# Routed experts beside a scan on one core: rows scattered unscaled, two rankings of the experts, and three late experts of the last block combined on chip

## The chip, the cores and the metric

The kernel runs on one core of a Trainium2 chip. A core has TensorE (PE in the profile; its weight loads are shown apart as PEld), VectorE (DVE), ScalarE (ACT), GpSimd (POOL) and SyncE (SP), each with its own instruction stream, and DMA queues. The metric is the device time of one execution in microseconds. Three runs of the kernel before took 468.14, 471.61 and 472.38 us, so the median is 471.61.

## The reference

The input is 16 sequences of 256 tokens with 128 features, 4,096 rows in all. Four sublayers follow one another, each on a layer norm without gains and added to its input:

```python
x = x + attention(_layernorm(x))          # layer 1
x = x + ffn(_layernorm(x))
x = x + selective_scan_block(_layernorm(x))  # layer 2
x = x + ffn(_layernorm(x))
```

The attention multiplies its softmaxed weights, summed over the keys, with v at the query's own place; these sums are 1, so what remains is a product with two matrices. The scan block keeps 16 states per feature over the sequence, with `delta` through a softplus, and ends with a matrix, a skip term `u * D` and a bias. The ffn is a mixture of eight experts of 128 x 512 and 512 x 128 with a relu between them. Each token goes to two:

```python
gate_logits = x @ gate_w
top_vals, top_idx = jax.lax.top_k(gate_logits, TOP_K)
top_w = jax.nn.softmax(top_vals.astype(jnp.float32), axis=1)
h = jax.nn.relu(jnp.einsum('td,edf->etf', x, w1))
expert_out = jnp.einsum('etf,efd->etd', h, w2)
```

and its output is the sum of its two experts' rows, weighted with `top_w`.

## The kernel before

The 4,096 rows are held on chip as eight blocks of 512 tokens (`xs_[b]`, four tiles of 128 tokens each). In what follows "layer 1" is attention, the first ffn and the scan (the *mixer*); "layer 2" is the second ffn. Layer 1 takes its blocks in the sets [0], [1], [2,3], [4,5], [6,7], layer 2 in [0,1], [2,3], [4,5], [6], [7].

For each set the ffn goes through four steps.

*Routing* (`choose`, `route`, L1156 and L1330): VectorE finds the two best experts of each token and their softmax shares `p`; small bf16 matmuls count tokens, so that each token gets a place in the list of its expert. Each expert has a *room* (`SLOTS`): n pieces of K rows. Then each token's row is normalized, multiplied with its share and written, once for each of its two experts, into a DRAM buffer `slots` at its place: ScalarE or VectorE makes `row` from x, and GpSimd scatters 128 rows with one indirect DMA (L880). Because the expert's relu commutes with a positive factor, the share may be applied to the input. Set [0] of layer 1 goes without DRAM: its rows are dealt to the experts by matmuls with marks (`spot`, `dealt`; tile `u` of `ramp` compared with places).

*Experts* (`experts`, L1389): for each expert the room is fetched (`xs<-slots`), transposed, multiplied with w1 (tiles `ps_b` and `ps_B` from `xsT`), put through the relu (`h`), multiplied with w2 (`ps_y`), transposed back (`yr`) and written to a DRAM buffer `ys`. Rows of the eight experts alternate in `slots` and `ys`, so that a room is read in pieces of 512 bytes.

*Collection* (`collect`, L1446): for each block GpSimd gathers each token's two rows (`yy<-ys,of`, L892, four gathers for each of the two), and VectorE or GpSimd adds them to x as a whole, 128x512.

*What follows*: the mixer in layer 1 (`arrive`), the transposed output to DRAM in layer 2 (`finish`).

In layer 2 the first set ranks the experts by load (`ranking`), so that the rooms can fall from the busiest expert to the least busy. The weights are loaded again from DRAM in that order, by registers that SP reads (`load_experts`, L934 to L940). In layer 1 all rooms of a set are equal.

The mixer (L1492) normalizes and transposes x to `u`, computes `delta`, runs the scans of the 16 states in four groups (exp and tanh on ScalarE, products and scans on VectorE, broadcasts of B and C by bf16 matmuls), and ends for each block with two matmuls into one sum: `wsd_s` (the output matrix times D) with u, 512 columns, and `wsh_s` with the scan's last 180 steps of both sequences, 360 columns.

The order of the instructions on each engine is fixed before the chip runs: all operations are jobs of a plan, with the duration that the plan believes, and a stored list of ranks (`ORDER`) and choices of engine decides which job goes next on which engine. On SP the order of the DMA issues is fixed in the same way; a DMA there that waits holds back those behind it. Where the plan leaves TensorE without work for 0.5 or more, it puts one matmul with a blank tile for every 0.26 of the gap (L1705): these *fillers* compute nothing.

After the last block the kernel tests whether a room was too small or the scan's cut was too short; then a general path computes all of it again, without routing.

Of the kernel before, what the change touches and what calls it, by code (L numbers as in the profile page):

```python
# [19 lines left out]
P = 128  # L20
# [12 lines left out]
    {  # L33
        "first": ((88, 2),) * 8,
        1: ((84, 2),) * 8,
        2: ((108, 3),) * 8,
    },
    {
        "first": ((126, 3), (112, 3), (108, 3), (98, 3), (96, 3), (88, 3), (126, 2), (117, 2)),
        1: ((98, 2), (91, 2), (88, 2), (80, 2), (84, 2), (75, 2), (70, 2), (128, 1)),  # L40
        2: ((126, 3), (117, 3), (110, 3), (104, 3), (108, 3), (96, 3), (90, 3), (126, 2)),
    },
)
RANKED = (2,)
UNIT = 2
JOIN = 2

COLD = 5.0
# [14 lines left out]
    "c-qZZ2V4_p|G(!F2uWCBZ^GVNMD}nMWhmmpRjsY4t)oufI_lQiswi$nt>RvFf>K)%!~%*UB1=HoJFEa1cmE`Jxw{}(`+wi}^LZ0U"  # L63
    "a?kVJZ+?H@-|v>G_^I*=>c6NNCEAl^pxer^W>rkfI9&R;>iv%8rd7`B9lu02joA1NUDGqgsne+5m*>sC|3s_)i)v%K>WE364%f`z"
    "G%9VWd>|BeK0IC08FfuyS$#TV!ssUsJvZ9pw@tBaV2TlOKM(^Ype&9CWvPXsXYyKG+Pu%zXlZI1Sm&A}IY4CALbDer*&iR4gwV&l"
    "%_}jzc_s5zX!X3PvIWf#4x)X!&c}M*s#~aW*_FM4<>R>>-Ss7LRsE&oXUE3!i@n2)%YK;$2Ux%Q=KJd&AzO97EXmqll<=(G$|n86"
    "dYcDRExkEyN=&Uj^@^>Aca=O|2u`0WZ*KkZPp*nx>bjin<VsZC<o=9uRhFUFl+z=MPhNm~zw4pXzFM^_s$-IHUykn8ElEaxc^26-"
    "@4I$-U9_@v4^`W~w0Z1KeP?YmwJLUVr{|Jk*2t*vvi=>escnr%S2%5T@YvyUd1cK_&1T~j6D^|8^}R6ZVc4@5r`2UVu#9lkK^d>j"
    "<5raWMYj1fEzYZOy26KDMUnzv7Ki#3$Js3MGeWdkH_RQX!$+g^SGwX*L0g)m*&ht^hr`B{m+-Z+MtiQ=%kQlyO?ID9`_|x>g>x4a"
    "7{0aWT9KvwE7Mny<Gx<_BC^rwXq|G-%~+*L?XOC-N_X*TlWs>d*t>6dr4MgmZ>V5Cdl#UwvuaJIa7A;6SkO9NyAy2)R#I*_c4irG"  # L70
    "f$}i1aA)c7s#VilXwygk=1!Yh4K5@zA4WBp!hdS2*QXZDe|&PBD<YV-*P?Y!iDl#0qE3S>ix*QK?M<<E=x(XAp(VMh1?XG@R;LUe"
    "^+r5mvX*|O{~BSeh+)#r_1}t5_Zhr&a6Vyi`WybF4oh}yO!N4+5htCOsU-6w+usb|b1Ki@BBPCK;{T?1ty+gYBRIVexWd-=;yaSJ"
    "&s)c$pQk1Mu(kK>{gXydj2^f9i*!A>vkJ$Aory7?vCXs9d*QbqY<=vPD_5viZHRw+xyi_Maei$clW%G}<<Bhkhz`r&MH-;Cg^e&a"
    "U3gYoEtvixd0S^(bWqX_ezZ?DQW4gCxKZW)U-sXiwFV<^9XWugj&I$OH!^<jINSI_Rp(0X8CAy1J2}<+XY8MsQOzx+FI`ck!)UF1"
    "r{3=xWR>+`>d7lshLx35&odZn7Zx}mrDnxJanplDErz>)?7F~R3+C+aA5-pJSJA{omZhmanOZhgkCAfdi0_(u)pB)q^G@34(G14f"
    "eS4#Xe51_BB9U#NK~YP9t>|iZM^tyo*>WS%F&D1MxJN(sPW#RtZCBBJZJ^)!epUT0n_AeiD}P#^{fyO-2NJ+a(?751T|Dt?cbC&s"
    "Vc(n$QTC>HM#at;b;t51I;SD3MmT%!f%h}4>PBvxuFe>3;@b3@A8^VmYfe%~m6J|SeG|jhc2S6Tkp)nnb$DNx$-9k@&62&})9eDh"
    "ScjD#Mm+6S`}*KmrOj)ty&MV-D)rOH_rKCv)^PRbMmOGYj!yTV8??Q`+N`UlY#O%f5B};74O>|C*7x@ozso+too$4EyDPAtJ-2Le"
    "uTEEI%<mI*o7jdlVWH_fj=;E{yK8^RlKf4p9e+HX@qI@>qK&dre+c0=@TMCTa6xyst-wJ;H>2N&$y}<c%!q`U@CUzomIp^G>DPJt"
    "S!x=E$jI-zmAMAtYp?dBF3J<a_^i}!9^FgHm{tEc#Gh9&w{A|0ef5VbPi>8y1=e34J|A%@QR|nJJQv~V+30jzx^DxA@33*RbCs>%"  # L80
    "ef3A`HOopwyjkjeHH}(F$Ieng4b!X;HExa5f1%a}jGt%hF>5F+ZFknJV%x@_61{ioY8P?EddV{*+HUb(fS#Qbt)^2r^(WJ`)UPYu"
    ")JFWl;98WeIb=8Tk2<=R1-&Pa79=`8w;g#um40nvvTte-sCm{D_|vkM$>|}6bRG!cYgMZ0^S*OreBm=TH+%Z~Jcp5~?Y_@P(9st@"
    "2CsX<E{?mh@~%t6aDJ(4L*w;>xy$qNjg9mfd=Ae^*L+-(bAJ8d=)3ycVdKZQ%egm9ODFqhX5N_LFyCI_K3f0nvJ^FDW!RAzPKVo+"
    "&IIVELnF5YsV!Rmvh`YcsoiL^-lwHm!S_vG?p9glT3%@%v(D~K^6D*%ik-FG(>9-*)PGiwXO`l5rF63Hy$X+bo)u_IOW1QRTiI}<"
    "<_VqfqH_^joC>Np-yO~piB@y!^DI<vt(p<a79|+4%EN6Q+BDz2GK+27_hV+{U*BnPFSKTUHNV=Vhjk($xUov;CwT7HHq%es;o@7v"
    "s~x8lM&||AjNuQ<wZ6Bmwd>bY8~1<UXj(W%Ur`$cXWJOv-;lnhYT8?FUx$uYp|x^`un9G&o1Iu;t!dRW&g^Bb=_0hyX(rG0_x5<J"
    "W}lxb*X~)HAE-1pB;BQ^LG!O|{!7wateXuPjy1g47G;AAOE#v|-`IO4l;JX=Le)SmG4aUQQQ6kXA%1z9t<NK0dmq^jAGBJpuKxgd"
    "eXkawFZ5$JMr2mlKB{8c=h)_Zy$KD=PPGs%xvk#g-~MD_9aH;}d%czM@ozmdc5X7%n7k(1V&fu#xkh5jB_tPq;C45@tIXzkaGgr;"
    "`U-V}elJ1K5|2t9!%F4Ie79N)zMgFdqAF5lr;az799pBdl=r?p=s{9t<;`CXoASO{t7VrlBRG@0J_1I0K8Wt`_lI$swmu6BI^+PG"
    "R<t`R#ilQeDPFoWaTfD_W-45&V`fle={DiT+;e$tuyA_JGv2os@98-1FqqaFKEJbL>3+MFs}kA@zjoxM2@bBZ-Zv|~*-qnO412%B"  # L90
    "Hrl?39I;U2Nl)*kc{(>WG8$)ax|gm~8_)17zHBvazRBVuOO~Pjb<fxgT5}Y$rBU13yY<|T>gT@6y{t2fvzNc1KieD~H?c3yIG5%1"
    "EZC;L<sGZu9pMPV16%ccCfxd9<XECrYvkB!<h1ocr=`%<`N@intL=VX)*h7_ooi=p!&4c>U}btmTfv<omWIQ-a$8N>Cfiq*;mz*K"
    "X~Rn9R^2?n+niWz_x`eL{ozpO&1-+YWLh^$VDQqHpSVriI0n@^F|pk#E1}=9&or)NWV*op*e;vXrU5-JJxh-3Fk{-vL_ZWd-(`H2"
    "k@>2&TjXi*rq>P$e>>}7fV!t%UxR&U@8s&d;UV$g>F5|2Zpc2S=4zO^Jm5y+3zK*Htk~qyL5(?+wC+!_Zq6Cy`MkJ=^V`TyeWuXt"
    "&YapiOGBTs*#<0g<ztSzO#Mb4*Oi?TS!SZ4o^E#ZOhD4zQ=R+|Ixbw%HSS}*_Wf~Z>nrHuK4p{B+fH~UE>nKqtaR_P_PR4V=)GIP"
    "!Ikr-C#gjoJ>T&4m`N)*+szxBUi?zstQE)^-*auA<Lrx}7Gn-|ZG9f9D$<H~iw)(J4uc)c&AfL9uaDPpx~_b%G&X4U1Ad5jy|0kt"
    "-q%m7eTec@?E3E4PPX$n(aU-rFg1Mb6W;3N3jQ<IiG33%{1O-0xc2P#Mc2LUH4C!)1d=i2$+S8jbn2MmrUfI44!n=6D`;&|bw8)y"
    "MfYYF)pRR$)vNK;YU^v8rn%{zpSh*DMQ>#O<%u3}gHdkWyZcHxnY}jZ*J4i7EpLtfqkWEhOIbWuuiJ~hV{K6Q^&if?00DY0hVOmz"
    "w(r2s*FMAf{wuvbzY9&%5hrHsZXcB!Frs-!vd?v~)$Q@#yhiOE3(d+F)HQFI-@S##Q8iU@>%DG>IK7Hv8*S0w$rzhkaXC6o)ji8s"
    "`!Bs^j7RVnPN~uUeqGnob@xW?s`toU?B})Hci%{(+x}N#%V$Pprx$y2*!ij>)2t(qr7We8OpgM4w#&%LI@|8^R%NLE{xFwj+K}6m"  # L100
    "b#UGJVz!Frr07J=%-<$(E^!5ZPiC$>cICE-+9D&MvC_q=&c?IIp#PomyfstNq`8xn_PPi{-i^Qb^B4icKWSfnWuEpshKGMXO-KBa"
    "=BoRm!22z7$df~xYih~RD4J0_uHf#=@y4}b4=0M=y}F&4Z()!27mYJDP#W|4r2qBc5k6+ZsmEp;lr-B_g}@On;%JxdtZy7=+QdGx"
    "yla*QO+TGe7qCPrt6tNs!1LsF+YX1c?FNBPU%_hnsIm6g1-Z(n%9a$4aLcXI(=D#wS?k^4&KOZ*`&&}y{2h1Nf(s*Ou)a7J-V;=5"
    "`P4q4-{LJlR5<M0=6>%|UzTqL+sN`e7sJ_KZg8@&@au7ONDB*z{gWFQUT1pQv}Vx+x9Hik#V7Rl+Z)hgxUIJA$4R$lKR?^2v3_#!"
    ">)PnR%R2jnzwLTu3Uu|kbtp<>T=OyQvM-&@w&$T@l}_3ZQ*NSLbH51^?E9;{t@f*o)tW*1N!vbj^|Lw3#=Yep4jt^mESpJxfC&!u"
    "_j<e<oHm85F<l%mC!pg^x#5;03HD#!nfc|W!Yv&~&3er&Hy#Y)c(sHwV#d^Ud=anS!QbqV|0JrT#@hFbW6e=28?RYgY;T}n^*esh"
    "+f#V-iGLybGSv_*tJ;;?#RTx?(>iSLS`GI|w-ybT=8a5-_S(Yg$bBX;2j0eVis|qA3g-E?KhJwV&Eu78T5)&z_y-)N`nxw$=*&I4"
    "nhaG+6Gw5t#PeFdh8BM?nN!+Kv}|TAVpYGdJksWFbWPdEPrax`*`nI_smPJjoW9V~)4$rh{Hwd?rzM>5KH{xeU~?{qv)X@bwaNGe"
# [553 lines left out]
def tile_layers(  # L662
# [43 lines left out]
    def room(k, blocks):  # L706

        first = blocks == routed[k - 1][0]
        return SLOTS[k - 1]["first" if first else len(blocks)]
# [1066 lines left out]
```

## Time and profile before

| | |
|---|---|
| median of three runs | 471.61 us |
| the profiled execution | 467.84 us, its span 466.1 us |
| TensorE busy | 447.0 us (96%), of which fillers 31.2 |
| VectorE busy | 345.6 us (74%) |
| ScalarE busy | 268.3 us (58%) |
| GpSimd busy | 311.8 us (67%); 128 gathers 125.5, 120 scatters 120.6 |
| DMA | 55.37 MB in 74,917 packets |
| granted TensorE clock | 0.994 |

The profile is one execution. Nearly all operations are recorded by one helper, so that they share the line L772, and are told apart by their tiles: `ps_y<-h,w_s` is a matmul that writes a `ps_y` bank from `h` and a weight. An f32 matmul stands as two records. A record of a matmul covers its whole pass through the array, and the passes overlap: how much one takes of TensorE's time is read from the distance of their starts, or from the chain, which counts each moment once. The chain of the last-ending work is followed back from the end, at each step to what released it.

### The profile page before, as it was taken

The page shows a single profiled execution, that of the slowest core. Times are in us where ns is not written, and L with a number is a line of the kernel's source. Part 1 is how long each engine was busy: PE and PEld are TensorE (multiplying, and loading weights), DVE is VectorE, ACT ScalarE, POOL GpSimd, SP SyncE. Part 2 cuts the span into 40 slices and gives each one's busy share as a digit, 9 for nine tenths or more (in the row PEclk, how much of TensorE's full clock was granted, in tenths as well). Part 3 has the DMA queues.
Part 4 walks back from the last instruction along what each step waited for, and adds up shares of the span by engine and source line. Part 5 has one row for each costly group of instructions (what it writes and reads, how often), then busy time and mean ns, then how long its engine had stood idle before and what let it go on. Part 6 is the DMA issues. An engine that isn't in the chain of part 4 may idle for free.

```text
span 466.1 us, 8797 instructions
## 1 busy us (share of the span) xinstructions
PE 447.0 (96%) x2670; PEld 355.8 (76%) x2670; DVE 345.6 (74%) x1229; ACT 268.3 (58%) x621; POOL 311.8 (67%) x482
## 2 busy tenths in 40 slices
PE   8999999999999999989997999989999999999994
PEld 6889998866766667665665777677678877999993
DVE  4799999778697878999999998996786931223420
ACT  2124443577576854995889496797735534343310
POOL 8188787777673761276866776836785477778662
PEclk9999999999999999999999899999999999999999
DMA  5974234632352423236644322144225333543251
GB/s 155 340 244 135 71 122 134 166 107 66 108 155 67 114 78 96 65 106 195 188 121 142 93 73 76 53 120 132 69 58 146 114 113 90 135 125 91 78 164 45
DMA packets 74917, 55.37 MB, mean 119 GB/s; under 512 B 8184, under 2 KB 66800, under 8 KB 74864
## 3 DMA queue, kind: packets, MB, share of 16 engines
q1 hardware_dynamic: 66640, 38.35, 28.5%
q0 software_dynamic: 7936, 16.27, 12.1%
q8 instruction: 23, 0.38, 0.4%
q14 instruction: 30, 0.25, 0.2%
q10 hardware_dynamic: 288, 0.13, 0.1%
HBM read 28.95 MB, written 25.77 MB: 117 GB/s over the span
## 4 chain that ended last, share of the span: by engine, by line
PE 72%; DVE 16%; ACT 4%; issue 3%; POOL 2%; DMA 1%; POOLq 0%; DVEq 0%; ACTq 0%
PE ps_b L772 25%; PE ps_y L772 24%; PE ps_B L772 21%; DVE x L772 3%; DVE ps_B L772 2%; DVE stats L772 2%; PE ps_y L1705 2%; POOL yy L892 2%; DVE w L772 1%; DMA yy<-ys,of 1%; DVE th L772 1%; ACT th L772 1%; DVE rt L772 1%; ACT decay L772 1%; DVE u L772 1%
## 5 line engine op out<-in xcount | busy, mean ns | idle before, releaser
L892 POOL DMA_INDIRECT yy<-ys,of x128 | 125.5, 980 | 64.4 <-issue 37.2
L880 POOL DMA_INDIRECT slots<-row,to x120 | 120.6, 1005 | 49.5 <-issue 19.4
L772 PE MATMUL ps_y<-h,w_s 128*128 128x324 f32 (+13 forms) x552 | 145.2, 382 | 0.0
L772 PE MATMUL ps_B<-xsT,w_s 128*128 128x324 f32 (+9 forms) x352 | 112.8, 442 | 0.8 <-DVE w L772 0.4
L772 PEld LDWEIGHTS ps_y<-h,w_s 128*128 128x128 f32 x552 | 90.4, 190 | 20.3 <-issue 1.3
L772 PEld LDWEIGHTS ps_B<-xsT,w_s 128*128 128x128 f32 x352 | 61.7, 191 | 23.8 <-issue 3.2
L772 ACT ACTIVATE h<-ps_B 128x648 f32<-128x648 f32 (+9 forms) x62 | 43.8, 707 | 33.5 <-PE ps_B L772 33.1
L772 PE MATMUL ps_b<-xsT,w_s 128*128 128x176 f32 (+9 forms) x288 | 54.8, 316 | 1.2 <-ACT yr L772 1.2
L772 PEld LDWEIGHTS ps_b<-xsT,w_s 128*128 128x128 f32 x288 | 44.1, 190 | 2.7 <-ACT yr L772 1.5
L772 ACT COPY yT<-ps_y 128x324 f32<-128x324 f32 (+14 forms) x52 | 18.8, 362 | 36.0 <-PE ps_y L772 35.2
L772 ACT ACTIVATE th<-later,lneps,ha_s 128x112 f32<-128x112 f32 (+13 forms) x85 | 39.1, 507 | 0.2 <-DVE th L772 0.2
L772 ACT ACTIVATE h<-ps_b 128x352 f32<-128x352 f32 (+9 forms) x47 | 22.3, 474 | 26.0 <-PE ps_b L772 24.1
L772 PE MATMUL ps_b<-ident,yT 128*108 128x128 f32 (+11 forms) x177 | 34.4, 274 | 0.7 <-ACT yr L772 0.7
L772 ACT COPY xsT<-ps_b 128x324 f32<-128x324 f32 (+15 forms) x52 | 19.1, 372 | 26.6 <-PE ps_b L772 25.3
L772 ACT ACTIVATE decay<-delta,nea 128x108 f32<-128x108 f32 (+13 forms) x85 | 31.7, 412 | 2.7 <-DVE delta L772 2.6
L1705 PE MATMUL ps_y<-blank,ones_d 128*128 128x128 f32 x232 | 31.2, 293 | 1.3 <-DVE blank L772 1.3
L772 DVE TENSOR_TENSOR_SCAN w<-decay,ps_B 128x360 f32<-128x360 f32 (+7 forms) x40 | 31.0, 802 | 1.3 <-ACT decay L772 0.5
L1705 PEld LDWEIGHTS ps_y<-blank,ones_d 128*128 128x128 f32 x232 | 30.0, 208 | 1.6 <-DVE blank L772 1.3
L772 ACT COPY yr<-ps_b 108x384 f32<-108x384 f32 (+13 forms) x50 | 21.3, 425 | 16.8 <-PE ps_b L772 16.8
L772 ACT ACTIVATE row<-x,mp,rp 128x128 f32<-128x128 f32 x63 | 28.1, 488 | 3.6 <-DVE rp L772 2.0
L772 PE MATMUL ps_b<-ident,xs 108*128 108x108 f32 (+13 forms) x186 | 29.7, 256 | 0.1
L772 DVE TENSOR_SCALAR h<-ps_B 128x648 f32<-128x648 f32 (+6 forms) x26 | 21.3, 819 | 11.1 <-PE ps_B L772 10.8
(207 smaller groups left out, 792.2 us busy)
## 6 DMA issues: line engine op xcount, KB each, us to landing
w_s<-in_w SPq DMA_DIRECT2D x32, 256.0 KB
xs<-slots SPq DMA_DIRECT2D x27, 162.0 KB
ys<-yr SPq DMA_DIRECT2D x27, 162.0 KB
slots<-blank SPq DMA_DIRECT2D x2, 1280.0 KB
xT<-in_xT SPq DMA_DIRECT2D x8, 256.0 KB
yy<-ys,of POOLq DMA_INDIRECT x128
out_T<-xnT SPq DMA_DIRECT2D x8, 256.0 KB
slots<-row,to POOLq DMA_INDIRECT x120
```

What stands on the lines that cost most here:

```text
L772: return lambda: f(*[real(x) for x in a], **{n: real(x) for n, x in k.items()})
L880: inst = nc.gpsimd.indirect_dma_start(out=real(out), out_offset=bass.IndirectOffsetOnAxis(ap=real(rows), axis=0), in_=real(in_), in_offset ...
L892: nc.gpsimd.indirect_dma_start(out=real(out), out_offset=None, in_=real(in_), in_offset=bass.IndirectOffsetOnAxis(ap=real(rows), axis=0),)
L1705: nc.tensor.matmul(out=spare, lhsT=ones_d.real(), rhs=blank.real(), start=True, stop=True,)
```

## The change

- The rooms of the experts are set one set at a time. The experts are ranked in set [2,3] of layer 1 as well as in the first set of layer 2; the sets that follow use that ranking. The rooms of one set stand one behind the other in `slots` and `ys`, each in one piece.
- The ranking's tables hold a start and an end for each room, on all partitions. A token past its room's end is sent to spare rows behind the rooms.
- The first matrix of each expert is multiplied with I - 1/128 after loading (`centre`), eight matmuls of 512 columns, and the centred w1 and w2 are stored to DRAM (`w1c`, `w2c`); both reloads come from there. SP reads all eight registers in one step.
- Rows are scattered as x itself. The share times the reciprocal deviation (`share`) is applied at the collection: the first expert's rows, and all of layer 2, tile by tile with `scalar_tensor_tensor`; in layer 1 the second expert's rows are multiplied with it by ScalarE (or VectorE), tile by tile, and then added in one piece.
- For the last block of layer 2 three experts (`LATE`) are neither written nor gathered. Four mark matrices with the shares are built, transposed, and multiply the experts' rows on TensorE into the transposed output (`marks`, `finish`).
- The mixer scales u by 2D and adds the scan to its last 180 steps, and one matmul of 512 columns follows.
- Block 0's reciprocal deviations come from a power on GpSimd; marks of the first set may be made on ScalarE by two activations.
- The believed durations of transfers and the stored order are others.

```diff
+RANKED = ((1, 2), (2, 0))
+LATE = 3
@@ def load_experts(q)
+                pw = bank("B", P, FF)
+                matmul(pw, centre, into[0])
+                copy(into[0], pw)
+                move(w1c[r], into[0], 4 * P * FF, took=0.5, turn="centred")
+                move(w2c[r], into[1].rearrange("p c d -> p (c d)"), 4 * P * FF, took=0.5, turn="centred")
...
+            for f, t, of in ((first, into[0], [w1c]), (second, into[1], [w2c])):
+                plan.job([("SP", 0.55, f)], [t], of, late=-4.0 * P * FF, turn="weights", after=[seen])
@@ def choose(blocks, k)
-        V.tensor_tensor(rp, p, r.unsqueeze(1).to_broadcast([P, 2, n]), ALU.mult)
-        V.tensor_tensor(mp, p, m.unsqueeze(1).to_broadcast([P, 2, n]), ALU.mult)
+        share = new(f"share{n}", [P, 2, n], bufs=3)
+        V.tensor_tensor(share, p, r.unsqueeze(1).to_broadcast([P, 2, n]), ALU.mult)
@@ class Group
         def part(self, t, r):
-            n, c = self.room[r]
-            return t[0 : NE * n * c].rearrange("(p c e) w -> e p c w", e=NE, c=c)[r]
+            _, c = self.room[r]
+            return t[self.starts[r] : self.ends[r]].rearrange("(p c) w -> p c w", c=c)
@@ def marks(q, f)
+        for t in range(NTT):
...
+            for i, v in enumerate((hot[t], other)):
+                V.tensor_scalar(v, tail, f[:, i, t : t + 1], q.share[:, i, t : t + 1], ALU.is_equal, ALU.mult)
+            V.tensor_tensor(hot[t], hot[t], other, ALU.add)
...
+                for t in range(NTT):
+                    transpose(pt[:, ts(t, P)], hot[t][:, at : at + 1 + C * (K - 1) : C], hold=[m] if t == 0 else ())
+                copy(m, pt)
@@ def route(q, blocks)
+        if not q.dense:
+            past = small("rest", n, NE)
+            V.tensor_tensor(past, at[:, 0:n], spread(lies[:, 1], n), ALU.is_ge)
+            V.scalar_tensor_tensor(at[:, 0:n], past, BIG, at[:, 0:n], ALU.mult, ALU.add)
...
-                    either(
-                        ("ACT", "activation", (r[:, t, :], xs_[b][:, t, :], AF.Identity),
-                         dict(bias=m, scale=w)),
-                        ("DVE", "tensor_scalar", (r[:, t, :], xs_[b][:, t, :], w, m, ALU.mult,
-                                                  ALU.add), {}),
-                        turn="row" if t == 0 else None,
-                    )
-                        q.slots, idx[:, i, lo + t : lo + t + 1], r[:, t, :], f"in{q.name}",
+                        q.slots, idx[:, i, lo + t : lo + t + 1], xs_[b][:, t, :], f"in{q.name}",
@@ def experts(q)
+            if r >= q.late:
+                q.made[r] = yr
+                continue
@@ def collect(q, b)
-            product(xs_[b], xs_[b], y, ALU.add)
+            if q.k == 1 and i == 1:
+                for t in range(NTT):
+                    w = q.share[:, i, lo + t : lo + t + 1]
+                    either(
+                        ("ACT", "activation", (y[:, t], y[:, t], AF.Identity), dict(scale=w)),
+                        ("DVE", "tensor_scalar", (y[:, t], y[:, t], w, None, ALU.mult), {}),
+                    )
+                product(xs_[b], xs_[b], y, ALU.add)
+                continue
+            for t in range(NTT):
+                V.scalar_tensor_tensor(xs_[b][:, t, :], y[:, t, :], q.share[:, i, lo + t : lo + t + 1],
+                                       xs_[b][:, t, :], ALU.mult, ALU.add)
@@ def mixer(blocks, r, m)
-            matmul(so, wsd_s, u[:, i], True, False, hold=[sos])
-            matmul(
-                so.rearrange("p (s l) -> p s l", l=L)[:, :, L - KM : L], wsh_s,
-                whole[:, NSEQ * i : NSEQ * i + NSEQ], False, True,
-            )
+            either(
+                ("ACT", "activation", (u[:, i], u[:, i], AF.Identity), dict(scale=skip2)),
+                ("DVE", "tensor_scalar", (u[:, i], u[:, i], skip2, None, ALU.mult), {}),
+            )
+            product(ends[:, own], ends[:, own], whole[:, own], ALU.add)
+            matmul(so, wsh_s, u[:, i], hold=[sos])
@@ def finish(blocks, q)
+                for r, yr in q.made.items():
+                    last = r == NE - 1
+                    if last:
+                        for t in range(NTT):
+                            matmul(pt[:, ts(t, P)], xs_[b][:, t], ident, False, False)
+                    for c in range(q.room[r][1]):
+                        end = last and c == q.room[r][1] - 1
+                        matmul(pt, yr[:, c], q.rowsT[r, c], first, end, hold=[o] if first else ())
```

## The prediction

> **What bounds the kernel now.** I read four views in this order: the head of the page (engine shares and the chain that ended last), the busy times by stretch, the timeline of the last 20 us, and the groups of instructions by form. The head first:
>
> ```profile
> span 466.1 us, 8797 instructions
> PE 447.0 (96%) x2670; PEld 355.8 (76%) x2670; DVE 345.6 (74%) x1229; ACT 268.3 (58%) x621; POOL 311.8 (67%) x482
> ...
> PE 72%; DVE 16%; ACT 4%; issue 3%; POOL 2%; DMA 1%; POOLq 0%; DVEq 0%; ACTq 0%
> ```
>
> TensorE holds 72% of the chain, VectorE 16%. But "96% busy" counts fillers: matmuls on a blank tile that the program issues where its own plan leaves TensorE idle. Here they are, with the other rows that I price from:
>
> ```profile
> L1705 PE MATMUL ps_y<-blank,ones_d 128*128 128x128 f32 x232 | 31.2, 293 | 1.3 <-DVE blank L772 1.3
> L772 DVE TENSOR_SCALAR row<-x,rp,mp 128x128 f32<-128x128 f32 x57 | 18.3, 353 | 0.1
> L772 DVE TENSOR_TENSOR x<-x,yy 128x512 f32<-128x512 f32 x20 | 14.1, 705 | 17.4 <-DMA yy<-ys,of 17.4
> L772 DVE SCALAR_TENSOR_TENSOR x<-ps_B,rstd,x 128x128 f32<-128x128 f32 x32 | 10.4, 344 | 3.5 <-PE ps_B L772 3.5
> ```
>
> An f32 matmul is two passes in the trace, so 232 rows are 116 fillers. Split by time, 60 passes stand before 30 us, 60 in the middle and 112 after 444 us. The third view is the chain in order of time, then the end of the timeline:
>
> ```profile
> 110.80 2.18 PE ps_B L772 x8
> 440.96 0.94 POOL yy L892
> 443.45 2.45 DMA yy<-ys,of
> 456.29 2.59 DMA yy<-ys,of
> ```
>
> ```profile
> 447.55 0.94 POOL L892 DMA_INDIRECT yy<-ys,of  x1 [1.90 <-DVE x L772]
> 459.00 0.69 DVE L772 TENSOR_TENSOR x<-x,yy 128x512 f32<-128x512 f32 x1 [9.02 <-DMA yy<-ys,of]
> 460.54 0.59 ACT L772 COPY xnT<-ps_b 128x512 f32<-128x512 f32 x1 [14.68 <-PE ps_b L772]
> ```
>
> Two things are to be seen. The eight passes at 110.80 are of 324 columns: 0.2725 us a pass, 0.841 ns a column. And the last expert's last matmul starts at 444.0; after it come its write, eight gathers 1.25 us apart (447.55 to 456.29), their landing, an add, four transposes, a copy and the output: 22.0 us in which TensorE has almost only fillers. Last, by stretch (columns: length, then busy time of PE, PEld, DVE, ACT, POOL, clock, DMA share, GB/s):
>
> ```profile
> 26.00:248.00 222.00, 217.74 (x1226) 164.46 (x1226) 196.91 (x739) 146.26 (x340) 150.31 (x203) 1.00 0.42 120
> 248.00:444.00 196.00, 191.94 (x1189) 157.15 (x1190) 128.66 (x393) 115.41 (x263) 136.47 (x170) 0.99 0.35 100
> 444.00:466.10 22.10, 15.19 (x135) 14.79 (x134) 3.37 (x5) 1.93 (x4) 10.16 (x11) 0.95 0.33 105
> ```
>
> So until 248 us (layer 1) TensorE and VectorE (89%) are both close to full; after that TensorE alone; then the tail.
>
> **The change part by part.** Durations are of the profiled execution, 467.84 us (span 466.1 and 1.7 around it). It lies under the median of 471.61.
>
> *Smaller rooms.* The rows that pass the experts fall from 10,528 to 9,609 in layer 1 and from 9,980 to 9,802 in layer 2: 1,097 fewer. A row passes eight f32 matmuls, 16 passes at 0.841 ns = 13.5 ns: 14.4 us (with the by-row sums, which move 128 columns whatever the room, counted). With fewer pieces, transposes save 1.8. All of it is TensorE work on the path.
>
> *Mixer's output.* Per block, two passes of 512 columns and two of 360 become two of 512. Eight blocks: 16 x 360 x 0.841 ns = 4.8 us less. In exchange VectorE or ScalarE scales u once a block, and VectorE (7) or GpSimd (1) adds the scan.
>
> *Centred weights.* Eight new matmuls of 512 columns, 16 x 0.43 = 6.9 us, six of them ahead of the first deal. TensorE has some 20 us of idle time and fillers before 30 us, waiting for VectorE's ranks, so I cost them at nothing; without that cover they are +6.9. The sixth weight load is the fifteenth large transfer on SP; the loads here go out 0.7 us apart, so it is there by some 15 us, and the first deal is at 25.9. GpSimd sets 64 more single columns, at 0.09 us: 5.8 us ahead of its tables' last, and the matrix `before` waits behind them. Its new power of four variances lies between 0.46 (a 128x128 addition) and 1.28 (128x512); I take 0.5. Against that the first set no longer normalizes rows or multiplies shares (GpSimd waited 10.1 us for shares). Start: 0, from -3 to +7.
>
> *Late experts.* For the last block only five experts are written and gathered; 144, 128 and 127 rows stay on chip. Behind the fifth expert, in TensorE's new order, lie 11.0 us of work: those three experts (7), the transposes of two blocks and four matmuls of 512 columns (3.4). All of it stands beside the same 22 us of gathers. The 16 new transposes of marks (1.8) are ahead of it, and 12 VectorE operations of 399 elements, near 0.55 each (copy rows of 384 elements take 0.55), where VectorE is 66% busy. If gathers were no longer the last, the 11 us would be on the path.
>
> Together: TensorE's work ahead of the last gathers was 391.1 us (matmuls by columns, as above) and becomes 372.0 with the centring, 365 without it: **-26 us** if the start hides it, -19 if not.
>
> *Unscaled rows.* 57 VectorE and 63 ScalarE row operations go; scatters read x itself. Up to 248 us these were 32 x 0.348 and 40 x 0.486. With them go three small operations per routing (the mean twice, its share); two that clamp to the room come (0.19 each). What comes late in their place: scaling at the collection. Layer 1, first expert: 32 scalar_tensor_tensor at 0.344 = 11.0. Second: 24 on ScalarE (0.486, from the row operations) and 8 on VectorE, then 8 whole adds (7 on VectorE, 0.72 each). Layer 1's VectorE therefore loses 11.1 + 6.5 (9 adds) and gets 11.0 + 2.8 + 5.0, 4.9 for the mixer's additions and scalings, 1.4 for centred copies and some 2 for the new ranking: about **+8 us on the engine that is 89% full there**. Each second expert's add also waits one ScalarE operation longer, 0.49 us, and behind tanh rows (0.5) in ScalarE's queue: at five mixers up to 5 us, hidden as long as experts of another set are left on TensorE. In layer 2 VectorE gets 64 x 0.344 less 11 adds, at 66% load: hidden. Table loads stay at 11.
>
> *Fillers as evidence.* The new order has 95: 23 at the start, 55 in the middle, 17 in the tail (before 30, 30, 56). So the program itself expects 25 more idle quarters in the middle, nearly all where the mixers of layer 1 stand: 25 x 0.224 = **+5.6**, which agrees with VectorE's +8; I take 2 more, **+8** in all.
>
> *Second ranking and reload.* 16 stores of 256 KB and 16 more loads pass SP in layer 1. The reload of layer 2 shows the price: its 16 loads were issued from 206.1 to 246.5, some behind TensorE's last use of the old weights (9.2 us of SP's waits). Behind a waiting load stand writes of results and fetches. I take 0, because the loads follow the experts of the second set one by one; the bound is the rival below. Fetches and writes now move 1,024 or 1,536 bytes in a row instead of 512: a gain or nothing, from 0 to -4 (the chain has 1% of DMA).
>
> Sum: 467.84 - 26 + 0 + 8 + 0 = 450. The runs of before lie 0.3 to 4.5 above the profiled one, so I say **452**.
>
> *A rule against it.* Gathers take 0.945 us in the median and 0.98 in the mean, so all that lengthens them is 128 x 0.035 = 4.5 us, as much again for scatters. The Trainium skill ("GPSIMD Engine Reference", Key points) says that GpSimd shares its SBUF interfaces with VectorE and contends with instructions that have two SBUF inputs. The change adds 96 of these and takes 20 (and 12 on GpSimd). By the rule 33 us of such holds replace 14, and GpSimd might lose up to 19 us; by the trace, where far more such holds cost both kinds of transfers 10 us, it is 2 or 3, off the path except beside the last eight gathers. I go by the trace.
>
> **The rivals.**
> 1. *VectorE sets layer 1.* For it: 89%, and the chain between 197 and 232 us runs through VectorE. Against it: TensorE has another set's work meanwhile. Then the rows and mixers of layer 1 bring nothing; left are 2.4 us in layer 2 and the 7 us of late experts, and up to 8 are lost: 459 to 466. An unhidden start (+7) ends in the same place.
> 2. *The reload stalls (slower).* In layer 1 the weights of the third set can go only after the second set's experts. 16 loads took 40 us in before; the second set's eight experts cover 8 x 168 x 13.5 ns = 18 us. If set three has to wait for the rest, 22 us come back: 450 + 22 = 472, up to 485 if results and fetches queue on SP behind the waits. It decides from the point where TensorE's input transposes in layer 1 wait for weights or fetches (0.0 to 0.1 us now). Against it: the new order still has experts of the first two sets and mixers there.
> 3. *Better still.* TensorE loses 22 us without fillers between 26 and 294 us, 8%. If longer DMA rows and a freer GpSimd (23 us of adds and deal rows less) shrink this by a third, 440 to 445.
> 4. *It doesn't hold.* If a room overflows, the general path runs after all (1,024 matmuls of 512 columns at 0.86 us, 880 us more). The reference's routing fills 294 of 297 rows at the closest: under 1 in 100.
>
> **How the numbers follow.** Forecast (445 to 458): 0.52. Rival 3: 0.10. Rival 1: 0.22, about half of it within 1% (463 to 472), which is about what a measurement of this kernel tells from no change. Rival 2: 0.15, all slower. So faster 0.75, same 0.10, slower 0.15. The range 440 to 472 leaves out rival 2 and the edge of 3.
>
> **What would show it.** Right: a span near 449; after the fifth expert's write eight gathers with matmuls beside them; layer 1's last mixers no later than now (294 us), with VectorE over 90% until then; what follows them shorter by some 20 us. Wrong: TensorE waiting at `w_s` or `xs` between 100 and 160 us; centring matmuls that end after 26 us; a tail over 15 us without real matmuls.

## The result, and the profile after

The changed kernel takes **590.4 us** in the median (584.0 to 593.7) beside 470.3 us for the kernel before. The ratio is 1.246, 95% interval 1.233 to 1.258. The forecast was 452 us, and the whole range (440 to 472) is missed. Two of the four runs fell in a slower state of the chip and are left out of the ratio, and on three of the six chips on which the experiments below ran, the kernel before itself took 627 to 656 us instead of 467 to 473, so runs from there are read only beside each other.

The head of the changed kernel's page, with the chain that ended last:

```profile
span 585.8 us, 8806 instructions
...
PE 465.9 (80%) x2652; PEld 372.0 (64%) x2652; DVE 368.4 (63%) x1304; ACT 248.1 (42%) x577; POOL 291.2 (50%) x535
...
PE   8899999793848948368993599979979499477794
...
PEclk9999999896859987869996599999998699699798
DMA  8955697221122111112742203232232123223131
...
PE 53%; DMA 26%; DVE 8%; issue 6%; ACT 3%; POOL 2%; SPq 1%; POOLq 0%; DVEq 0%; ACTq 0%
```

Before, DMA had 1% of the chain; now it has 26%. No engine is full. The TensorE row is close to full for seven slices of 14.6 us and then full of holes, and from there on the DMA engines are mostly busy for one to three tenths: everything waits for transfers, and the transfers use little of what there is. The granted clock falls in the holes, to 0.5 and 0.6; it is 0.894 in the mean. That is a consequence: in the profiled run of the kernel below that mends the transfers it is 0.999, and 0.987 to 0.999 in all its eight runs.

Who waits is in the groups of instructions (columns: busy, mean ns of one, idle time just before and what ended it). First a line of the kernel before, then two of the changed one:

```profile
L772 PE MATMUL ps_b<-ident,xs 108*128 108x108 f32 (+13 forms) x186 | 29.7, 256 | 0.1
```

```profile
L780 PE MATMUL ps_b<-ident,xs 94*128 94x94 f32 (+25 forms) x182 | 32.9, 276 | 54.6 <-DMA xs<-slots 51.6
L780 DVE SCALAR_TENSOR_TENSOR x<-yy,share,x 128x128 f32<-128x128 f32 x96 | 32.2, 349 | 54.2 <-DMA yy<-ys,of 54.1
```

The first matmul of an expert, which transposes the fetched room, waited 0.1 us in all before the change. Now TensorE stands 51.6 us there, and VectorE 54.1 us for gathered rows (17.4 before, at the adds), which can only be gathered when the results are written. Three stretches of the trace show what the DMA engines do meanwhile (columns: length, busy time of PE, PEld, DVE, ACT and POOL, granted clock, DMA share, GB/s):

```profile
215.00:220.00 5.00, 0.00 (x0) 0.00 (x0) 0.00 (x0) 2.94 (x3) 1.07 (x2) 0.60 0.07 25
280.00:285.00 5.00, 4.88 (x20) 3.44 (x20) 4.67 (x20) 4.63 (x14) 4.10 (x9) 1.00 1.00 335
541.00:545.00 4.00, 0.00 (x0) 0.00 (x0) 0.04 (x1) 0.00 (x0) 0.00 (x0) 0.84 0.07 23
```

In the first and the last, TensorE and VectorE do next to nothing and the DMA share is 0.07 at 23 to 25 GB/s. One engine of sixteen is 0.0625. Between them the weights of layer 2 are loaded at a share of 1.00 and 335 GB/s: the engines are there, but the transfers that everyone waits for run on one of them.

The raw events of the trace say the same for each transfer. They hold one event for each DMA engine whose part has landed and, unless all sixteen take part, one more that comes ahead of them (an event is missing here and there). Counted for the fetches `xs<-slots` of rooms with three tokens in a row (1,536 bytes):

```
rows of the room   engines that land   us from issue to the last landing (changed kernel)
108                12                  5.4 to 9.2
126                14                  8.2
96                 16                  10.0
98                 14                  13.7 to 16.8
95                  5                  10.1 to 11.4
87                  3                  11.0
94                  2                  7.0 to 14.2
106                 2                  6.4 to 12.6
89                  1                  12.3 to 15.3
97                  1                  14.7 to 14.8
103                 1                  12.1 to 17.3
107                 1                  23.0
```

The number of engines is the largest number up to 16 that divides the rows. How long a transfer takes isn't settled by that number alone: the rooms of 98 rows run on 14 engines and land later than most, as they are fetched among those on one or two engines. In the stretch from 215 to 220 us two fetches are under way, one of 98 rows (issued at 205.9 us, landed at 220.7) and one of 97 (212.1 and 226.9), and still the DMA share is that of one engine: what is left of both is on the same one. In the kernel before every room had a good number of rows (108, 126, 112, 96, 88, 84 and so on), its fetches of 108 rows landed within 2.8 to 4.8 us, and nothing in its profile could show what a bad one costs. The new, tighter rooms have 103, 106, 97, 95, 94 or 89 rows. The Trainium skill states the rule ("DMA: Bandwidth & Descriptors", section "Why a DMA increments its semaphore by 16 and not by 1"): a DMA is split over the largest k up to 16 that divides the slowest dimension of both access patterns, and the semaphore gets 16 - k at once. The events here agree for each size in the table. The page adds that the lowest-numbered k engines are taken. That the slow transfers all queue on the same engine fits that, and the 12 to 23 us of rooms whose packets take 7 (103 packets of 65 ns), but no run here shows an engine's number.

An estimate from these packets (65 ns for 1,536 bytes, 46 for 1,024, 27 for 512): if every transfer has a part on that engine, it carries 157 us of fetches and 156 us of writes.

### The profile page after: what moved, and what is told of

Read it like the earlier page. It is cut to its first block, busy times and chain, and to the rows that moved or that the text cites. A ratio compares the mean times of both kernels' runs of the same rounds, so it can differ in the third digit from the quotient of the medians.

```text
span 585.8 us, 8806 instructions
## 1 busy us (share of the span) xinstructions
PE 465.9 (80%) x2652; PEld 372.0 (64%) x2652; DVE 368.4 (63%) x1304; ACT 248.1 (42%) x577; POOL 291.2 (50%) x535
## 4 chain that ended last, share of the span: by engine, by line
PE 53%; DMA 26%; DVE 8%; issue 6%; ACT 3%; POOL 2%; SPq 1%; POOLq 0%; DVEq 0%; ACTq 0%
PE ps_y L780 18%; PE ps_b L780 17%; DMA xs<-slots 16%; PE ps_B L780 15%; DMA yy<-ys,of 3%; DMA ys<-yr 3%; PE ps_y L1843 3%; DMA slots<-blank 2%; POOL yy L915 2%; DMA out_T<-xnT 2%; DVE w L780 1%; DVE ps_B L780 1%; DVE x L780 1%; SPq L780 1%; DVE th L780 1%
## 5 line engine op out<-in xcount | busy, mean ns | idle before, releaser
L780 PE MATMUL ps_y<-h,w_s 128*128 128x176 f32 (+21 forms) x528 | 137.0, 383 | 14.6 <-DVE h L780 9.9
L903 POOL DMA_INDIRECT slots<-x,to x120 | 121.2, 1010 | 42.3 <-issue 25.5
L780 PE MATMUL ps_B<-xsT,w_s 128*128 128x282 f32 (+17 forms) x336 | 113.6, 465 | 11.7 <-DVE h L780 9.6
L780 PE MATMUL ps_b<-ident,xs 94*128 94x94 f32 (+25 forms) x182 | 32.9, 276 | 54.6 <-DMA xs<-slots 51.6
L780 DVE SCALAR_TENSOR_TENSOR x<-yy,share,x 128x128 f32<-128x128 f32 x96 | 32.2, 349 | 54.2 <-DMA yy<-ys,of 54.1
L780 ACT ACTIVATE h<-ps_B 128x564 f32<-128x564 f32 (+17 forms) x55 | 36.8, 672 | 62.4 <-PE ps_B L780 60.7
L780 PE MATMUL ps_b<-xsT,w_s 128*128 128x176 f32 (+12 forms) x304 | 60.6, 327 | 0.3 <-issue 0.3
L780 PE MATMUL ps_y<-w_s,h 128*122 128x128 f32 (+6 forms) x232 | 37.0, 296 | 2.6 <-DVE h L780 2.4
L780 PE MATMUL ps_b<-ident,yT 128*88 128x128 f32 (+20 forms) x169 | 34.6, 276 | 4.2 <-DVE h L780 3.7
L780 PEld LDWEIGHTS ps_y<-w_s,h 128*122 128x122 f32 (+6 forms) x232 | 33.6, 206 | 6.0 <-DVE h L780 2.6
```

The source lines that it names most:

```text
L780: return lambda: f(*[real(x) for x in a], **{n: real(x) for n, x in k.items()})
L903: inst = nc.gpsimd.indirect_dma_start(out=real(out), out_offset=bass.IndirectOffsetOnAxis(ap=real(rows), axis=0), in_=real(in_), in_offset ...
```

## The experiments

**1. Wide places.** The rooms keep their 103 or 94 rows for the computation, but each lies in a place of 104 or 96, and fetch and write move the whole place. TensorE's work and the order of all jobs stay.

```diff
+WIDER = {
+    83: 84, 86: 88, 87: 88, 89: 90, 94: 96, 95: 96, 97: 98, 103: 104, 106: 108, 107: 108,
+    109: 110, 115: 120, 122: 126, 123: 126, 124: 126, 127: 128,
+}
-                ends.append(ends[-1] + n * c)
+                ends.append(ends[-1] + laid(n) * c)
-                x = new("xs", [P, CMAX, P], bufs=XS)[0:K, 0:C]
-                move(x, q.part(q.slots, r), 4 * N * P, took=0.55, turn="fetch")
+                KF = laid(K)
+                x = new("xs", [P, CMAX, P], bufs=XS)[0:KF, 0:C]
+                move(x, q.part(q.slots, r, KF), 4 * N * P, took=0.55, turn="fetch")
-            move(q.part(q.ys, r), yr, 4 * N * P, took=0.55, key=f"out{q.name}")
+            move(q.part(q.ys, r, KW), kept, 4 * N * P, took=0.55, key=f"out{q.name}")
```

(`laid` looks a size up in `WIDER`; `kept` is the whole tile, `KW` its wide size.) Two half measures go with it, round fetches alone and round writes alone, and one change of a single number in the kernel *before*:

```diff
-        2: ((108, 3),) * 8,
+        2: ((107, 3),) * 8,
```

> The changed kernel with its tables alone laid out wider: a room of 103 rows lies in a place of 104, one of 94 in 96, one of 122 in 126 and so on, and the fetch and the write of a room move the whole place. TensorE, VectorE and ScalarE do what they do in the changed kernel, the written order of jobs is the same. Theory A (the number of rows decides how many of the 16 DMA engines carry a transfer: in the changed kernel's trace a room of 103 rows lands with one event beside the opening one and takes 12 to 17 us from issue to landing, one of 108 with twelve events): packets of 65 ns for 1536 bytes, 46 for 1024 and 27 for 512 put 157 us of fetches and 156 us of writes on the most loaded engine, and 29 and 32 us once the places are wide; fetches land within 2 to 6 us, TensorE's wait for xs falls from 51.6 us to under 5, and the time falls to 445 to 470 us, near the forecast. Rival B (the reloads of layer 1, or the written order, hold SyncE's queue): 570 to 600 us, as nothing of that is touched. Rival C (ScalarE's scaling and VectorE's adds in layer 1): 570 to 600. Rival D (the contiguous layout, pieces of 1536 bytes in place of 512): 570 to 600, as the pieces stay as long.

> The changed kernel with its tight layout, the fetches alone made to read a round number of rows (the rows past the room are those of the next one and are not used); the writes are as they were. Theory A: the most loaded engine keeps 156 us of writes and 29 us of fetches in place of 313, the fetches still queue behind the writes there: between the changed kernel and the one with both wide, 490 to 545 us. Rivals B, C and D: 570 to 600.

> The wide layout with the writes moving the whole place, and the fetches only the room's own 83 to 127 rows. Theory A: 157 us of fetches and 32 us of writes on the most loaded engine, and each slow fetch (7 us of packets alone) stands right ahead of TensorE: 490 to 560 us, not below the kernel with fetches alone made round. Rivals B, C and D: 570 to 600.

> The kernel before with one number changed: the rooms of the last three sets of layer 1 have 107 rows in place of 108, three tokens each. It saves 72 rows of TensorE's work, about 1 us at 13.5 ns. Theory A: 107 has no divisor up to 16 but 1, so that each of the 24 fetches and 24 writes moves 321 pieces of 512 bytes at 27 ns, 8.7 us, on one engine: 416 us of packets where the stretch from 83 to 250 us has 167; 650 to 750 us in all. If the cause is anything that the change brought (reloads, order, scaling, layout), 468 to 472 us.

These four first fell on a chip where the kernel before took 634.8 us. Beside it they took 642.1 (1.011 times, 1.002 to 1.020), 659.2, 663.6 and 838.5 us. The first of them was run on another chip:

> The kernel of p_both once more: there the kernel before itself took 630 to 641 us, a third longer than the 468 to 472 us beside the changed kernel, with stretches in which TensorE, VectorE, ScalarE and SyncE all stand still for no wait that the trace names, so that its times can't be laid beside the changed kernel's 590 us. Where the kernel before takes 468 to 472 us again: theory A 445 to 470 us, a ratio of 0.95 to 1.0; rivals B, C and D 570 to 600 us, a ratio of 1.21 to 1.27.

It took 642.1 us beside 633.8, so the condition of its expectation was not met. What the changed kernel takes beside them was the next run:

> The changed kernel itself once more, beside a kernel before that takes 627 to 641 us on the chips that the experiments run on, in place of 468 to 472. Theory A: it stays slower than the kernel with wide places (642 us) by what the fetches and writes cost on few engines, 60 to 140 us: 700 to 780 us, a ratio to the kernel before of 1.10 to 1.25, and both half measures (659 and 664 us) lie between the two. Rivals B, C and D, for which the width of the places is nothing: 635 to 650 us, as with wide places.

That run fell on an undisturbed chip, so its expectation, made for the other kind, can't be judged: 587.4 us beside 470.9 (1.247, 1.240 to 1.253). The same four kernels on undisturbed chips:

> The kernel with wide places for fetch and write, on a chip on which the kernel before takes 468 to 472 us (the changed kernel took 587 us on such a chip, 1.247 times the kernel before). Theory A: 445 to 470 us, 0.95 to 1.0. Rivals B, C and D: 570 to 600 us, 1.21 to 1.27.

> The tight layout with round fetches and the writes as they were. Theory A: 490 to 545 us; rivals B, C and D: 570 to 600.

> Wide places with round writes and the fetches as they were. Theory A: 490 to 560 us, not below the round fetches alone; rivals B, C and D: 570 to 600.

> The kernel before with rooms of 107 rows in place of 108 in the last three sets of layer 1, on a chip on which the kernel before takes 468 to 472 us (where that took 635 us, this took 838). Theory A: 24 fetches and 24 writes of 321 pieces of 512 bytes at 27 ns on one engine, 416 us of packets: 650 to 750 us. Otherwise 468 to 472.

| | us (median) | to the kernel before |
|---|---|---|
| changed kernel | 587.4 | 1.247 (1.240 to 1.253) |
| round writes alone, two runs | 527.2 and 537.1 | |
| round fetches alone, two runs | 501.4 | 1.069 (1.061 to 1.077) |
| wide places, both round | **464.1** | **0.990 (0.987 to 0.993)** |
| before | 469.5 to 470.9 | 1 |
| before, 107 rows for 108, one run | 728.1 | |

All four lie where theory A put them, and nowhere near the rivals' 570 to 600 (468 to 472 for the last). The page of the kernel with wide places:

```profile
span 462.0 us, 8812 instructions
...
PE 432.9 (94%) x2652; PEld 348.5 (75%) x2652; DVE 369.0 (80%) x1308; ACT 247.3 (54%) x577; POOL 293.9 (64%) x535
...
PEclk9999999999999999999999999999999999999999
```

In it a fetch of 104 rows lands on 13 engines in 3.1 to 5.6 us, one of 96 on 16 in 2.2 to 5.6. Its line for the transposes shows that no fetch is waited for any more:

```profile
L790 PE MATMUL ps_b<-ident,xs 94*128 94x94 f32 (+25 forms) x182 | 28.5, 251 | 0.0
```

With round fetches alone the same group still waits, behind the writes on the loaded engine:

```profile
L790 PE MATMUL ps_b<-ident,xs 94*128 94x94 f32 (+25 forms) x182 | 30.8, 266 | 14.2 <-DMA xs<-slots 14.2
```

And with round writes alone:

```profile
L790 PE MATMUL ps_b<-ident,xs 94*128 94x94 f32 (+25 forms) x182 | 31.5, 267 | 27.8 <-DMA xs<-slots 26.7
```

The fetches are the larger share, 86 us if mended alone; the writes bring 50 to 60 alone and 37 after the fetches.

The kernel with 107 rows holds nothing of the change: old layout, one ranking, scaled rows, old order. One row less in 24 rooms costs 258 us. The head of its page:

```profile
span 726.4 us, 8934 instructions
...
PE 496.8 (68%) x2736; PEld 387.7 (53%) x2736; DVE 354.0 (49%) x1241; ACT 264.1 (36%) x605; POOL 310.0 (43%) x484
...
DMA  7843511022101000210110133432222323334432
```

Its list of TensorE's waits (in all, times, longest) begins with the fetches, and the DMA row is at two tenths or less from the sixth slice to the twenty-third, until the last of these sets is through:

```profile
PE ps_b L772 <- DMA xs<-slots: 101.4, 15, 19.1
```

**2. What is left of the forecast.** With the transfers mended the kernel is at 464.1, not 452. The stretches between four marks (the first matmul of the first mixer, of the eighth and of the tenth routing, the end), in us:

| | before | changed | wide places |
|---|---|---|---|
| start to first mixer | 100.1 | 101.4 | 103.2 |
| to the eighth routing (layer 1, and some of layer 2) | 200.9 | 291.6 | 211.4 |
| to the tenth routing | 70.1 | 85.6 | 67.3 |
| to the end | 95.0 | 107.2 | 80.1 |

The end is 14.9 us shorter, but the stretch to the eighth routing is 10.5 longer. That routing is layer 2's third, so the stretch isn't layer 1 alone. By the columns of the first expert matmuls, 8,850 rows pass the experts in it before and 8,815 with wide places, of which 1,884 and 2,720 are layer 2's. So what the smaller rooms save in layer 1 is filled with layer 2's rows inside the stretch, and behind it 7,082 rows are left instead of 8,096. Layer 1 itself, up to the last mixer's output, ends 7.5 us later than before (365.3 for 357.8 us), 3.1 of which the first mixer has already. The same stretch by engine, before and with wide places (columns as above):

```profile
100.10:301.00 200.90, 195.39 (x1012) 135.28 (x1011) 178.29 (x519) 151.97 (x336) 131.79 (x170) 0.99 0.36 105
```

```profile
103.20:314.60 211.40, 196.76 (x1121) 147.63 (x1120) 189.77 (x548) 146.66 (x333) 129.12 (x168) 1.00 0.34 102
```

VectorE has 11.5 us more to do in it and is as full as before, 89 and 90%. TensorE is without a real matmul for 25.6 us instead of 12.5 (gaps between matmuls, fillers counted as gaps), for as many rows: these 13.1 us are what is lost. Two experiments put VectorE's load up and down. One gives 15 relus of over 256 columns, 11.3 us in layer 1, to ScalarE:

```diff
+            if job.n in eased and way[0] == "DVE":
+                way = next(w for w in job.ways if w[0] == "ACT")
```

> The kernel with wide places (464 us), in layer 1 the relus of more than 256 columns that VectorE does given to ScalarE, at the same place in the written order: some 14 us (19 at 0.76 in the trace of the kernel with wide places) leave VectorE, some 13 us (0.67 each) come to ScalarE, which is 60% busy in layer 1. There VectorE is busy for 253.6 of 286.3 us (89%), in the kernel before for 246.4 of 275.0 us (90%). Theory E (with the transfers mended it is VectorE that sets layer 1, so that the smaller rooms and the mixers bring nothing there): 450 to 459 us, the last routing of layer 2 some 6 to 12 us earlier than 381.9. Rival F (what is left is the gathers' and the collection's latency, or the written order): 461 to 467 us.

The other does each scaling of a first expert's rows in layer 1 twice:

```diff
+            engine.scalar_tensor_tensor(idly, y, w, x, *ops)
+            return engine.scalar_tensor_tensor(out, y, w, x, *ops)
```

> The kernel with wide places, in layer 1 each of the 32 scalings of a first expert's rows done twice on VectorE, once into a spare tile: 32 at 0.344, 11.0 us more of VectorE's work, nothing else changed and the order the same. Theory E: 471 to 477 us. Rival F: 463 to 467, as an engine that doesn't set the end hides it.

Measured: 471.8 us (1.0036, 1.0006 to 1.0065) with less on VectorE, 469.2 us (0.999, 0.996 to 1.002) with more. Neither theory got either. These runs fell on another chip and at a lower granted clock (0.990 and 0.991 in the mean, 0.994 with wide places), so I give two differences to the wide places, one of the medians and one by the ratios to the kernel before. 11.0 us more on VectorE cost 5.1 or 4.2, so its load counts, by less than half. But 11.3 us less there made the kernel 7.7 or 6.4 us slower. The relus keep their place in the written order and now stand in ScalarE's queue, and TensorE waits longer for them, first with wide places, then here:

```profile
PE ps_B L790 <- ACT h L790: 1.1, 2, 0.9
```

```profile
PE ps_B L790 <- ACT h L790: 3.6, 7, 0.9
```

That is 2.5 us of the loss; the rest is not traced.

Next, whether TensorE's rows count in layer 1 at all, the second expert's way, and the simplest cure:

```diff
-        ((108, 3), (99, 3), (94, 3), (90, 3), (89, 3), (87, 3), (128, 2), (122, 2)),
+        ((108, 3), (108, 3), (108, 3), (108, 3), (108, 3), (108, 3), (128, 2), (126, 2)),
-        ((106, 3), (103, 3), (98, 3), (97, 3), (95, 3), (94, 3), (94, 3), (89, 3)),
+        ((108, 3),) * 8,
```

(the second line twice)

> The kernel with wide places (464 us), the last three sets of layer 1 with rooms of 108 rows nearly throughout, as in the kernel before: 779 rows more to compute, at 13.5 ns 10.5 us of TensorE's work, all in layer 1; the transfers move 108 rows on twelve engines. Theory G (in layer 1 the engines wait for each other at the hand-offs, with or without the rows, so that smaller rooms bring nothing there): 463 to 468 us. Rival H (TensorE's work still decides in layer 1): 471 to 477 us.

```diff
+                    instead[plan.jobs[-1].n] = lambda: None
                 product(xs_[b], xs_[b], y, ALU.add)
...
+                def added(x=xs_[b], y=y, w=q.share[:, i, lo : lo + NTT]):
+                    for t in range(NTT):
+                        nc.vector.scalar_tensor_tensor(
+                            x[:, t].real(), y[:, t].real(), w[:, t : t + 1].real(), x[:, t].real(),
+                            ALU.mult, ALU.add,
+                        )
...
+                instead[plan.jobs[-1].n] = added
...
-            way[2]()
+            instead.get(job.n, way[2])()
```

(The four scalings of a block are left out, and at the place of the add in one piece VectorE does `added`.)

> The kernel with wide places, in layer 1 the second expert's rows scaled and added by VectorE in four operations a block, as the first expert's are: 24 scalings of 0.40 leave ScalarE, 9.6 us, 8 of 0.28 and seven whole adds of 0.69 leave VectorE and one of 1.27 GpSimd; 32 operations of 0.35 come to VectorE, net 4.1 us more there. If the way through ScalarE's queue and the add in one piece are what holds layer 1: 457 to 462 us. If VectorE's load weighs as in the run with the doubled scalings (5.1 us for 11.0): 465 to 467 us.

The third is the changed kernel with other numbers in `SLOTS`, those of `WIDER` (115 down to 112):

> The changed kernel with the rooms themselves grown to the next size with a large divisor (103 to 104, 94 to 96, 122 to 126 and so on; one, 115, down to 112) and nothing else: 162 rows more to compute, 2.2 us of TensorE's work, and no clearing of tiles at the start, which costs VectorE some 2 us with wide places. Theory A: 462 to 467 us, as with wide places; the first deal at 26.7 us again, not 28.7. Rivals B, C and D: 570 to 600.

All three fell on a disturbed chip (before: 649.5 us): 759.9 us (1.170, 1.161 to 1.179), 666.7 (1.026, 1.018 to 1.034) and 706.4 (1.088, 1.078 to 1.097). Wide places were at 1.011 on such a chip. The first and the third have a flaw of their own: `SLOTS` also feeds the durations from which the program plans its order, and with other sizes the stored ranks gave another order, with 692 and 194 filler passes more than the changed kernel has. So the grown rooms, which were expected to equal the wide places, did not, and why was not told apart. The first two were repeated, the first with the planned durations of the kernel with wide places written in, so that every engine's order is the same:

> The kernel with wide places (464 us), the last three sets of layer 1 with rooms of 108 rows nearly throughout, now with every engine's instructions in that kernel's own order, fillers included (in the run before, the plan made for other sizes came out in another order, with 692 filler passes more). 779 rows more to compute, 10.5 us of TensorE's work at 13.5 ns, all in layer 1. Theory G (in layer 1 the engines wait for each other at the hand-offs, so that smaller rooms bring nothing there): 463 to 468 us, a ratio of 0.985 to 1.0. Rival H (TensorE's work still decides): 471 to 477 us, 1.0 to 1.02.

> The kernel with wide places, in layer 1 the second expert's rows scaled and added by VectorE in four operations a block; 9.6 us leave ScalarE, net 4.1 us come to VectorE. If the way through ScalarE's queue and the add in one piece hold layer 1: 457 to 462 us, a ratio of 0.97 to 0.985. If VectorE's load weighs as in the run with the doubled scalings: 465 to 467 us, 0.99 to 0.995.

With the rooms of 108 rows: 473.8 us (1.0076, 1.0044 to 1.0109). 779 rows cost 9.7 us by the medians and 8.3 by the ratios, 12.5 or 10.6 ns a row. Rival H was right: TensorE's rows count in layer 1 for most of their price, and theory G falls. With the second expert's rows scaled and added by VectorE alone: 467.6 us (0.994, 0.991 to 0.997), 3.5 more than with ScalarE and the add in one piece by the medians, 1.9 by the ratios, whose intervals overlap. So ScalarE's way and the add in one piece are not what holds the kernel up; that they are a gain is likely, but not clear of the scatter.

**3. The version that beats both.** The wide places bring a clearing of four tiles at the start, 1.6 us of VectorE ahead of the blank tile; the last kernel does it behind the first two tiles, where VectorE has nothing to do.

> The kernel with wide places (464 us), the clearing of four tiles at the start (1.6 us of VectorE, ahead of the blank tile that the first fillers and sums need) moved behind the first two tiles, into VectorE's 5 us without work. If the start's delay goes through to the end: the first deal at 26.7 instead of 28.7 us and 461 to 463 us, a ratio of 0.98 to 0.987. If later waits take it up: 463 to 465.

463.5 us (0.990, 0.982 to 0.997): the first deal is at 27.0 us instead of 28.7 and the span 460.8 instead of 462.0, but the medians differ by 0.6 us, less than the runs scatter. This or the first version is about 1% faster than the kernel before.

## Why the prediction was wrong, point by point

*What bounds the kernel*: right, by the runs above: added rows cost 8 to 10 of their 10.5 us and added work of VectorE 4 to 5 of its 11, and so the reading "TensorE, with VectorE beside it in layer 1" holds.

*Smaller rooms* (-14.4 us of TensorE's work): the size was right. TensorE's real passes, by columns, take some 385 us in the changed kernel, where I had summed 383, and experiment r_full2 gives 10.6 to 12.5 ns a row where I had 13.5. What the step left out is that a room's size is also the shape of two transfers. I priced 97 and 103 rows as fewer matmul columns and looked no further.

*Fetches and writes* ("a gain or nothing, from 0 to -4"): **this is the step that failed.** It measured +123 us (587.4 - 464.1). I looked at the length of the pieces, which did grow, and took it for the only thing that changes in a transfer. The evidence against it was half in sight: rooms of 108 rows in the old table, which twelve divides, became 103, 97, 94 and 89, and the trace held landing events that count engines. The range went by bounds from rows of the old trace, in which no transfer of this kind occurs; "0 to -4" had no upper bound behind it at all. The skill's rule quoted above states how a transfer is split; I had not connected it with the rooms.

*Late experts* (-26 us with the rest ahead of the last gathers): the mechanism came as described. In the kernel with wide places the last eight gathers run beside experts' matmuls (timeline):

```profile
441.27 0.94 POOL L925 DMA_INDIRECT yy<-ys,of  x1 [3.19 <-DVE x L790]
...
443.80 0.94 PE L790 MATMUL ps_b<-xsT,w_s 128*128 128x128 f32 x6
...
447.96 1.88 PE L790 MATMUL ps_b<-xT,yr 72*128 72x512 f32 x4
...
450.00 0.94 POOL L925 DMA_INDIRECT yy<-ys,of  x1 [0.30 <-issue]
```

I had 11.0 us of work for the three experts and what goes with them beside the gathers. From the last mixer's output to the end, TensorE is without a real matmul for 11.2 us instead of 19.2, so 8.0 of them show. That the stretch from the tenth routing is 14.9 us shorter is not these experts' doing alone: it also holds 901 rows fewer (3,475 for 4,376), as more of them are done before it. By the signs that I had named, one failed and one came in part: the last mixer begins 11 us later (305.8 for 294.4 us) where it was to be no later, and what follows it is 15 us shorter where I had some 20.

*Centring at the start* (0, from -3 to +7): the first deal is at 26.7 us in the changed kernel, 25.9 before. Right.

*Reload* (0): right. With wide places no wait of TensorE for `w_s` is in the list, and up to the first mixer the changed kernel is level (101.4 against 100.1).

*Unscaled rows* (+8 us on VectorE in layer 1, +8 in time): for the whole of layer 1, from the first deal to the eighth routing, VectorE has 253.3 us where it had 246.4, +6.9, near the load that I had summed, though this stretch holds 836 more rows of layer 2 than before. (My own mark for layer 1, 248 us, lies in such a mixed stretch too.) The time was under-sized: TensorE's pauses between first mixer and eighth routing grew by 13.1 us. That is 5 more than the 8 taken; with the start (first mixer 3.1 us later, some 1.7 of it from the experiment's own clearing) and the 3 us that the tail fell short it makes 11 of the 14 us by which the profiled run of the wide places (463.8) lies above my sum of 450. It is pauses more than work: real matmuls cover 410.4 us of the span where they covered 419.0, about the 8 us less that I had summed, and the rest of the span grew from 47.1 to 51.6. Why the middle has these pauses is not settled. VectorE's load alone isn't it, nor ScalarE's part in the second expert's rows. What is left is the order itself: its plan, by the program's own durations, ends 8.3 us sooner than the old one, where my sum had 18. That is argued, not shown, as I tried no other order.

*GpSimd and the shared interface*: gathers took 0.945 us in the median before and 0.946 with wide places, the mean 0.98 and 0.99. Going by the trace was right; the 19 us that the rule would allow are not there.

*The rivals.* Rival 1 named 459 to 466 us for a kernel whose layer 1 brings nothing, and 464 lies in it, but its mechanism, VectorE setting layer 1, holds by less than half. Rival 2 was the only one on the other side, and its sign was the one that I had named: TensorE waiting at `xs` between 100 and 160 us. But its cause, reloads and SyncE's queue, is not what happened, and its price ended at 485. Rivals 3 and 4 did not come. A rival "the transfers themselves become slow" was missing.

## What to carry to other kernels

Before a size is tightened, ask what else has that size as its shape. The number of rows, that is of partitions, of a transfer decides how many DMA engines carry it: keep it at a number with a divisor near 16, and where the computation wants 103 rows, let the transfer move 104. A DMA share of 0.07 (one engine of sixteen is 0.0625) and some 25 GB/s while every engine waits for a transfer is the sign that it runs on one engine.

A stored order is made for its durations: after a change of sizes, compare orders before times.

## What the runs showed that I had not expected

- One row less, 107 for 108, in 24 rooms of the kernel before: 470.2 to 728.1 us. Each of these fetches lands on one engine, 12 to 23 us after its issue, in place of 2.8 to 4.8 on twelve.
- Slow transfers delay quick ones. Fetches of 98 rows of three tokens, on 14 engines, took 13.7 to 16.8 us in the changed kernel and 2.5 to 3.5 with wide places; one of 96 rows on 16 engines took 10.0, and 2.2 to 5.6 with wide places. They, too, have a part on the engine that the others wait for.
- In layer 1 no engine quite hides another: 10.5 us more on TensorE cost 8 to 10, 11.0 more on VectorE 4 to 5, and moving 11.3 from VectorE to ScalarE cost 6 to 8.
